# Two-layer graph attention and a transformer layer on one core: the first 1024 nodes' terms made and spread before the mask turns

## The chip, the cores and the metric

The kernel runs on one core of a Trainium2 chip. The metric is device microseconds of one execution. The kernel before has a median of 3264.52 us over three runs (3263.38 to 3267.57).

## The reference, cut to what matters

There are 4096 nodes with 256 features (`x`) and one 4096 x 4096 integer adjacency matrix (`adj`, 64 MB). Two graph attention layers come first, then one transformer layer whose attention uses the same matrix as its mask.

```python
Wh  = jnp.einsum('nd,hdo->hno', x, W)            # W: 8 heads, 256 x 32
src = jnp.einsum('hno,ho->hn', Wh, a[:, :O])
dst = jnp.einsum('hno,ho->hn', Wh, a[:, O:])
e = jax.nn.leaky_relu(src[:, :, None] + dst[:, None, :], 0.2)
alpha = jax.nn.softmax(jnp.where(adj[None] > 0, e, NEG_INF), axis=-1)
out = jnp.einsum('hnm,hmo->hno', alpha, Wh)      # then elu, and x is added
```

The scores of a graph attention layer depend on two numbers per node and head: a source term and a destination term. Because the leaky ReLU has two slopes, the kernel needs for each pair of nodes only the sign of (source term + destination term) and the mask bit. It multiplies sign and mask matrices with values scaled by exponentials of the destination term.

## The kernel before, in words

**Groups.** A graph attention layer is done in 64 groups (`l`, `nb`, `p`, `g`): two blocks `nb` of 1024 destination rows, four pairs of heads `p`, eight column groups `g` of 512 nodes (4 tiles of 128). TensorE's main loop (L1351) multiplies, for each of 8 row tiles and 4 column tiles, the comparison tiles `t8` and the mask tile with the values `vst[g]`.

**What a group needs.** `compare(i)` makes `t8` for group i two groups ahead: four column tiles times two heads, by VectorE (L1086) or ScalarE (L1084), and then one VectorE instruction over 128 x 2048 words, `mask()` (L1099), which puts the mask into them. `compare` reads `s_b`, a tile in which the source terms of 1024 rows are repeated on all 128 partitions. `s_b` comes from `s_fetch` (L1060), two DMAs of 512 KB that read 4 KB rows of the DRAM tensor `s_d` 128 times each. `s_d` is written by `term_rows` (L1031), four DMAs per 512 nodes, after `g_sr` (L1028).

**What makes the terms.** `preparation(l, q)` handles 512 nodes: `features` (L965, L968) transposes the rows, `values(t)` (L978 to L1010) multiplies with `w_ext` and makes the terms and the scaled values, `split(t)` (L1016 to L1019) writes `vst` as two f16 halves with GpSimd's subtraction, and `term_rows` follows. Since a block has 1024 rows, `s_b` for the first group needs `preparation(0, 0)` and `preparation(0, 1)`. `weights_of(l)` (L921 to L941) loads the weights and makes the two term columns of `w_ext`.

**The mask.** `mask_load` (L858) fetches 512 KB of `adj`, `mask_clip` (VectorE, L867) makes bytes of it, `mask_turn` (TensorE L890, ScalarE L892) transposes it, and every second turn is stored to DRAM for later use (L895). Eight such units are the first two column groups; groups 0 to 5 then turn four units each. The loads use three buffers (`g_adj`), so a fourth load waits for a clip.

**Order.** The order on TensorE, ScalarE and VectorE is that of the program, and in `begin()` SyncE's (SP) too. Outside `begin()` a scheduler places SP's DMAs, and can put later ones between those of `begin()`. All DMAs here are issued by SP, in order. In the main loop `beside` places side work between the row tiles of a group. `Norms.__init__` (L1383) loads five small vectors, element by element, as the first DMAs of the program.

Of the kernel before, what the change touches and what calls it, by code (L numbers as in the profile page):

```python
# [751 lines left out]
def graph_attention(  # L752
# [79 lines left out]
    pt = turn_bank([P, HB], F32)  # L832
    nc.tensor.matmul(pt[:, 0:2], once, tiny, start=True, stop=True)
    nc.vector.tensor_scalar(checks.column(), pt[:, 0:1], 2.0**-20, None, op0=ALU.is_equal)
    bits = rows_p.tile([P, P], F16, name="g_rows")
    seen = keep.tile([P, 3], F32, name="g_seen")
    for at, pattern in ((0, 0x38), (32, 0x8000), (64, 0x3880), (96, 0x80)):
        nc.vector.memset(bits[at : at + 32].bitcast(U16), pattern)
# [73 lines left out]
    layers = []  # L912
    coming_rows = {}

    def weights_of(l):

        w, a = weights[l]
        L = Layer()
        L.w_ext = keep.tile([P, DC, D + 2 * H], F32, name="g_w_ext")
        for c in range(DC):  # L920
            nc.sync.dma_start(  # L921
                L.w_ext[:, c, 0:D].rearrange("p (h o) -> p h o", o=O),
                w[:, c * P : (c + 1) * P, :].rearrange("h p o -> p h o"),
            )
        a_sb = ep.tile([P, H, 2, O], F32, name="e_terms")
        nc.sync.dma_start(
            a_sb.rearrange("p h s o -> p (h s o)"), spread(a, [[0, P], [1, H * 2 * O]])
        )
        wa = ep.tile([P, DC, H, O], F32, name="e_x")
        values_ = L.w_ext[:, :, 0:D]  # L930
        terms = L.w_ext[:, :, D:].rearrange("p c (k h) -> p c k h", k=2)
        for k in range(2):
            nc.vector.tensor_tensor(
                wa,
                values_.rearrange("p c (h o) -> p c h o", o=O),
                a_sb[:, :, k, :].unsqueeze(1).to_broadcast([P, DC, H, O]),
                op=ALU.mult,
            )
            nc.vector.tensor_reduce(terms[:, :, k, :], wa, AX.X, ALU.add)
        nc.vector.tensor_scalar(terms[:, :, 1, :], terms[:, :, 1, :], -1.0, None, op0=ALU.mult)  # L940
        nc.vector.tensor_scalar(values_, values_, UP, None, op0=ALU.mult)  # L941
        L.terms = keep.tile([P, 2, NT, H], F32, name=f"g_terms{l}")
        L.negd = L.terms[:, 1]
        L.r = keep.tile([P, NT, H], F32, name=f"g_r{l}")
        L.tops = keep.tile([P, NT], F32, name=f"g_tops{l}")
        L.ft = {}
        layers.append(L)

    def rows_ahead(l, q):
        if q < NG:  # L950
# [3 lines left out]
    def preparation(l, q, bank, first=False):  # L954

        L = layers[l]
        held = {}

        def features(c):

            if c == 0:
                L.ft[q] = stage_p.tile([P, DC, HB], F32, name="g_ft", tag="stage")
            pt = bank()
            for t in range(G):
                nc.tensor.transpose(  # L965
                    pt[:, t * P : (t + 1) * P], coming_rows[l, q][:, t, c * P : (c + 1) * P], ident_f
                )
            nc.scalar.copy(L.ft[q][:, c, :], pt)  # L968
            if c == DC - 1:
                del coming_rows[l, q]  # L970
                if (l, q) != (0, 0) and (l == 0 or q + 1 != NG - 2):
                    rows_ahead(l, q + 1)

        def values(t):
            at = G * q + t
            pv = bank()
            for c in range(DC):
                nc.tensor.matmul(  # L978
                    pv[:, : D + 2 * H],
                    L.ft[q][:, c, t * P : (t + 1) * P],  # L980
                    L.w_ext[:, c, :],
                    start=(c == 0),
                    stop=(c == DC - 1),
                )
            nc.scalar.copy(
                L.terms[:, :, at, :], pv[:, D : D + 2 * H].rearrange("p (k h) -> p k h", k=2)
            )

            big = some.tile([P, 2, H], F32, name="g_big", bufs=4)
            for i, scale in enumerate((-1.0, -LRELU)):  # L990
                nc.scalar.activation(big[:, i, :], pv[:, D + H : D + 2 * H], AF.Exp, scale=scale)
            nc.scalar.activation(L.r[:, at, :], pv[:, D : D + H], AF.Exp, scale=LRELU - 1.0)
            nc.vector.tensor_reduce(
                L.tops[:, at : at + 1], pv[:, :D], AX.X, ALU.max, apply_absolute_value=True
            )

            if l == 0:
# [12 lines left out]
            nc.vector.tensor_scalar(prod[:, :, :, O:], by_head, UP, None, op0=ALU.mult)  # L1010

        def split(t):
            part = held.pop(t).rearrange("p h i v -> p h (i v)")
            halves = vst[q][:, t].rearrange("p h (k v) -> p h k v", k=2)
            if first or t % 2 == 1:
                nc.scalar.copy(halves[:, :, 0, :], part)  # L1016
            else:
                nc.vector.tensor_copy(halves[:, :, 0, :], part)  # L1018
            nc.gpsimd.tensor_tensor(halves[:, :, 1, :], part, halves[:, :, 0, :], op=ALU.subtract)  # L1019

        def term_rows():
# [6 lines left out]
            nc.scalar.copy(sr, pr)  # L1028
            for t in range(G):
                at = (G * q + t) * P  # L1030
                nc.sync.dma_start(s_d[l][:, at : at + P], sr[t * H : (t + 1) * H])  # L1031
# [200 lines left out]

    def begin():

        rows_ahead(0, 0)
        weights_of(0)
        rows_ahead(0, 1)

        units = own[: 2 * 2 * NW]
        del coming[: len(units)]  # L1240
        for k, u in enumerate(units):
# [3 lines left out]
            elif k == 7:  # L1245
                place = t_p.tile([P, 2, G * P], I32, name="t8")
            mask_load(*u, place)
        for q in range(2):
            for k, step in enumerate(preparation(0, q, spare_bank, True)):
                step()  # L1250
                if q == 0 and k in (3, 5, 7, 9):
                    mask_clip(*units[(k - 3) // 2], load=False)
                if q == 1 and k in (2, 4, 6, 8):
                    mask_turn(*units[k // 2 - 1])
                    mask_clip(*units[k // 2 + 3], load=False)
        s_of[0, 0, 0] = s_fetch(0, 0, 0)
        load_ahead(3)
        for k in range(4, len(units)):
            mask_turn(*units[k])
            mask_clip(*turns[0][k - 4])  # L1260
        for i in range(2):
            for step in compare(i):
                step()

    ev = acc = None
    ordered = {mybir.EngineType.PE, mybir.EngineType.Activation, mybir.EngineType.DVE}
# [2 lines left out]
        begin()  # L1269
    for i, (l, nb, p, g) in enumerate(groups):  # L1270
        if l + 1 < NL and nb == 1 and p == 0 and g == NG - 1:
            weights_of(l + 1)
        fetches(i)


# [15 lines left out]
        if i + 2 < len(groups):  # L1291
            steps = compare(i + 2)
            beside(steps[:-1], 0.25 if made else 0.0, 0.95)
            beside(steps[-1:], 0.96, 1.0)
        if i >= len(groups) - NG:
            mine = [step for at, step in handed if at == g]
            beside([lambda step=step: step(lambda: turn_bank([P, HB], F32)) for step in mine], 0.0, 0.9)
# [75 lines left out]
class Norms:  # L1373


    def __init__(self, nc, pool, small, ident, vectors):

        self.nc, self.small, self.ident = nc, small, ident
        self.sb = {}
        for name, src in vectors.items():  # L1380
            self.sb[name] = pool.tile([P, src.shape[0] // P], F32, name=f"n_{name}")
            with nc.allow_non_contiguous_dma(reason="one small vector"):
                nc.sync.dma_start(self.sb[name], src.rearrange("(c p) -> p c", p=P))  # L1383
        self.eps = pool.tile([P, 1], F32, name="n_eps")
        nc.vector.memset(self.eps, LN_EPS)

    def mean(self, xs):
        nc = self.nc
# [55 lines left out]
class Ahead:  # L1444
# [6 lines left out]
        self.xs, self.hn, self.held = {}, {}, {}  # L1451

    def weights(self, bank=None):
        self.w = []
        for c in range(self.D // P):
            self.w.append(self.rows_p.tile([P, self.w_qkv.shape[1]], F32, name="g_adj", bufs=3))
# [540 lines left out]
```

## Time and profile before

| | us |
|---|---|
| median of 3 runs | 3264.52 |
| the profiled execution's own time | 3265.68 |
| its span in the trace | 3263.9 |
| first matmul of the main loop (L1351) | 60.89 |
| stretch 60 to 157: groups 0 to 5, with `preparation` of q = 2 to 7 beside them | about 97 |
| stretch 160 to 840: the rest of graph attention layer 1, TensorE 40.00 of 40 us busy from 200 on | about 680 |

The profiled execution is 1.2 us above the median. A timeline line gives start, duration, engine, line, operation and, in brackets, how long the engine had been idle before it and what released it. SPq is SP's DMA queue; its durations are those of the issue, not of the transfer. A line of the windows view gives busy time of each engine within the stretch, with the number of instructions, and at the end TensorE's granted clock, the DMA engines' share and GB/s.

### The profile page before, as it was taken

To read this page: it belongs to the slowest core of one execution; us is meant where nothing else is said; L and a number is where in the kernel's file an instruction comes from. 1 tells how busy PE (TensorE), PEld (TensorE's weight loads), DVE (VectorE), ACT (ScalarE), POOL (GpSimd) and SP (SyncE) were. 2 spreads that over 40 slices of the span, in tenths; PEclk is the share of its full clock that TensorE was granted. 3 is DMA by queue.
4 is the path that set the end of the run, shared out by engine and by line. 5 is a ranking of instruction groups with operands and counts; after the bars stand their busy time and mean duration, and the time that the engine had idled before them with its cause. 6 is when DMAs were issued, how large, how long until landed. Compare 5 with 4: busy or idle time off the path is not lost.

```text
span 3263.9 us, 139140 instructions
## 1 busy us (share of the span) xinstructions
PE 3098.8 (95%) x64076; PEld 2713.6 (83%) x64076; DVE 2805.1 (86%) x3102; ACT 2703.2 (83%) x3305; POOL 1176.4 (36%) x536
## 2 busy tenths in 40 slices
PE   4899999999889999999988999999999999997999
PEld 3799999999879999999965888888888888885666
DVE  5899999998879999999965999999999999994121
ACT  4799999999779999999974888888888888884332
POOL 1300000000220000000001898899988998893110
PEclk7999999999999999999999999999999999998999
DMA  6666555430311212121136010101011010004200
GB/s 209 193 206 219 159 171 172 145 93 22 99 42 34 93 54 93 37 59 47 38 104 159 14 40 14 39 20 33 27 27 49 11 43 14 20 8 119 70 33 27
DMA packets 210306, 249.30 MB, mean 76 GB/s; under 512 B 87792, under 2 KB 131056, under 8 KB 209712
## 3 DMA queue, kind: packets, MB, share of 16 engines
q1 hardware_dynamic: 209712, 240.31, 24.5%
q8 instruction: 503, 8.24, 1.1%
q14 instruction: 91, 0.75, 0.1%
HBM read 197.80 MB, written 42.47 MB: 74 GB/s over the span
## 4 chain that ended last, share of the span: by engine, by line
PE 44%; ACT 4%; DVE 3%; DMA 2%; issue 1%; POOL 0%; SPq 0%; POOLq 0%; DVEq 0%; ACTq 0%
PE u_ps L1668 14%; PE u_av L1686 14%; PE u_dn L1686 8%; PE misc L1874 3%; ACT t L1084 2%; PE misc L1611 2%; PE misc L1858 1%; DMA u_xres<-rows 1%; PE misc L1630 1%; DVE t L1086 1%; DVE t L1099 1%; PE misc L1432 1%; ACT ln_square L1399 0%; POOL u_xres L1817 0%; PE misc L1822 0%
## 5 line engine op out<-in xcount | busy, mean ns | idle before, releaser
L1351 PE MATMUL bank<-vst,t 128*128 128x132 f16 x16384 | 1451.3, 219 | 54.6 <-DVE t L1099 54.6
L1759 POOL TENSOR_TENSOR u_both<-u_e 128x1024 f32<-128x1024 f32 x448 | 1052.3, 2390 | 933.8 <-DVE u_e L1677 931.8
L1351 PE MATMUL bank<-vst,mask 128*128 128x66 f16 (+1 forms) x10296 | 1345.9, 206 | 0.0
L1084 ACT ACTIVATE t<-s_b,g_terms 128x1024 int8<-128x1024 f32 x1231 | 1318.8, 1155 | 30.9 <-PE bank L1351 21.6
L1351 PEld LDWEIGHTS <-t 128*128 128x128 fp8e4 x16384 | 1184.3, 97 | 69.1 <-DVE t L1099 59.5
L1677 DVE SCALAR_TENSOR_TENSOR u_e<-u_mask,u_ps 128x1024 f32<-128x1024 uint8 x1024 | 1165.8, 1213 | 9.8 <-ACT u_ps L1675 6.3
L1675 ACT ACTIVATE u_ps<-u_ps 128x1024 f32<-128x1024 f32 x1024 | 1030.1, 1009 | 141.5 <-PE u_ps L1668 46.0
L1351 PEld LDWEIGHTS <-mask 128*128 128x128 fp8e4 x10296 | 902.9, 98 | 0.0
L1099 DVE SCALAR_TENSOR_TENSOR t<-mask,t 128x2048 int32<-128x2048 int32 x256 | 591.1, 2309 | 79.9 <-ACT t L1084 69.5
L1668 PE MATMUL u_ps<-u_q,u_k 128*32 128x512 f16 x8192 | 636.0, 382 | 11.7 <-DVE u_e L1677 11.0
L1686 PE MATMUL u_av<-u_e,u_v 128*32 128x128 f32 x16384 | 601.9, 273 | 0.0
L1686 PEld LDWEIGHTS u_av<-u_e,u_v 128*32 128x32 f32 x16384 | 487.4, 110 | 130.5 <-issue 1.2
L1086 DVE TENSOR_SCALAR t<-s_b,g_terms 128x1024 fp8e4<-128x1024 f32 x817 | 582.6, 745 | 0.0
L1019 POOL TENSOR_TENSOR vst<-g_prod,vst 128x528 f16<-128x528 f32 x32 | 38.9, 1232 | 775.8 <-DVE vst L1018 756.8
L1686 PE MATMUL u_dn<-u_both,u_ones 128*32 128x128 f32 x7168 | 279.6, 273 | 0.0
L1668 PEld LDWEIGHTS <-u_k 128*32 128x32 f16 x8192 | 228.3, 95 | 57.8 <-issue 16.2
L1686 PEld LDWEIGHTS u_dn<-u_both,u_ones 128*32 128x32 f32 x7168 | 212.1, 110 | 41.3 <-issue 0.4
L1865 ACT ACTIVATE u_hid<-misc,n_b 128x512 f32<-128x512 f32 x64 | 42.7, 682 | 149.5 <-PE misc L1858 149.4
L1881 DVE TENSOR_TENSOR u_xres<-u_xres,misc 128x256 f32<-128x256 f32 x32 | 13.5, 421 | 121.1 <-PE misc L1874 121.1
L1874 PE MATMUL misc<-u_w,u_hid 128*128 128x256 f32 x512 | 111.8, 379 | 0.0
L1858 PE MATMUL misc<-ln_cols,u_w 128*128 128x512 f32 x256 | 111.2, 592 | 0.0
L1874 PEld LDWEIGHTS misc<-u_w,u_hid 128*128 128x128 f32 x512 | 96.7, 190 | 13.3 <-issue 0.5
(146 smaller groups left out, 1921.3 us busy)
## 6 DMA issues: line engine op xcount, KB each, us to landing
g_adj<-in_adj_dram SPq DMA_DIRECT2D x123, 512.0 KB
mask<-mask SPq DMA_DIRECT2D x128, 256.0 KB
s_b<-s_d SPq DMA_DIRECT2D x64, 512.0 KB
u_mask<-mask SPq DMA_DIRECT2D x32, 512.0 KB
mask<-stage SPq DMA_DIRECT2D x48, 256.0 KB
rows<-e_x SPq DMA_DIRECT2D x32, 256.0 KB
half_d<-u_halves SPq DMA_DIRECT2D x32, 256.0 KB
u_q<-half_d SPq DMA_DIRECT2D x32, 256.0 KB
```

The source lines that it names most:

```text
L1084: nc.scalar.activation(to.bitcast(I8), s, AF.Sign, bias=negd, scale=-1.0)
L1086: nc.vector.tensor_scalar(to, s, negd, -1.0, op0=ALU.is_ge, op1=ALU.mult, saturate=False)
L1099: nc.vector.scalar_tensor_tensor(both, m32.unsqueeze(1).to_broadcast(list(both.shape)), SIGNS, both, op0=ALU.bitwise_or, op1=ALU.bitwise_and,)
L1351: nc.tensor.matmul(to, left, right, start=k not in opened, stop=last)
L1611: nc.tensor.matmul(pq, wq_sb[k][:, i * D + c * P : i * D + (c + 1) * P], hn[:, k, :], start=(k == 0), stop=(k == DC - 1),)
L1668: nc.tensor.matmul(ps[r * O : (r + 1) * O, j, :], k_st[:, h, at : at + O], q_st[:, h, :], start=True, stop=True,)
L1675: nc.scalar.activation(ps, ps, AF.Exp, scale=SCALE)
L1677: nc.vector.scalar_tensor_tensor(e, mask, 0.0, ps, op0=ALU.not_equal, op1=ALU.mult)
L1686: nc.tensor.matmul(to[j * O : (j + 1) * O, at], lefts[j], es[j // 2][:, j % 2, at], start=first and part == 0, stop=last and part == PARTS ...
L1759: nc.gpsimd.tensor_tensor(both, es_of[i - 1][u], es_of[i][u], op=ALU.add)
L1858: nc.tensor.matmul(ph, w1_sb[:, k, f * P : (f + 1) * P], hn[:, k, :], start=(k == 0), stop=(k == DC - 1),)
L1874: nc.tensor.matmul(po[:, :D], hid[:, f, at : at + P], w2_sb[:, f, :], start=(f == 0), stop=(f == FC - 1),)
```

## The change

- `weights_of(l)` becomes `weights_load(l)` (the DMAs, the attention vector first) and `weights_steps(l)` (five VectorE steps, whose products go to a `g_prod` tile and no longer to `e_x`). In layer 1 the five steps are placed one each into groups 0 to 4 of `nb` = 1, `p` = 1; before, all six instructions stood at the start of the last group of `p` = 0.
- `Norms` loads its five vectors in `load()`, called from `Ahead.weights`.
- The test pattern `bits` has its own buffer and no longer one of the two `g_rows` buffers. The rows of q = 0 and q = 1 are loaded one after the other, ahead of the mask loads; those of q = 2 after `s_fetch`.
- `begin()` runs both `features` first, then the weight steps, then the `values` and `split` steps of q = 0 and q = 1 with four clips between them and both `term_rows`, then `s_fetch`. Four mask turns with four clips, `compare(0)`, four turns with four clips, and `compare(1)` follow. The values of q = 1 use `g_prod` tiles (two buffers).

```diff
-    bits = rows_p.tile([P, P], F16, name="g_rows")
+    bits = keep.tile([P, P], F16, name="g_bits")
...
-        rows_ahead(0, 0)
-        weights_of(0)
+        weights_load(0)
+        rows_ahead(0, 0)
         rows_ahead(0, 1)
...
-        for q in range(2):
-            for k, step in enumerate(preparation(0, q, spare_bank, True)):
-                step()
-                if q == 0 and k in (3, 5, 7, 9):
-                    mask_clip(*units[(k - 3) // 2], load=False)
-                if q == 1 and k in (2, 4, 6, 8):
-                    mask_turn(*units[k // 2 - 1])
-                    mask_clip(*units[k // 2 + 3], load=False)
+        first, second = (preparation(0, q, spare_bank, True) for q in range(2))
+        for step in first[:DC] + second[:DC]:
+            step()
+        for step in weights_steps(0):
+            step()
...
+        for step in value[0][:2]:
+            step()
+        for k in range(2):
+            clip(k)
+            value[0][2 + k]()
+        row[0]()
+        for k in range(4):
+            value[1][k]()
+            part[0][k]()
+            if k < 2:
+                clip(2 + k)
+            if k > 1:
+                part[1][k - 2]()
+        row[1]()
         s_of[0, 0, 0] = s_fetch(0, 0, 0)
+        rows_ahead(0, 2)
+        for k in range(4):
+            turn(k)
+            if k < 2:
+                part[1][2 + k]()
+            clip(4 + k)
         load_ahead(3)
+        ahead = turns[0]
+        for step in compare(0):
+            step()
         for k in range(4, len(units)):
-            mask_turn(*units[k])
-            mask_clip(*turns[0][k - 4])
-        for i in range(2):
-            for step in compare(i):
-                step()
+            turn(k)
+            mask_clip(*ahead[k - 4])
+        for step in compare(1):
+            step()
...
         if l + 1 < NL and nb == 1 and p == 0 and g == NG - 1:
-            weights_of(l + 1)
+            weights_load(l + 1)
...
+        if l + 1 < NL and nb == 1 and p == 1 and g < 5:
+            if g == 0:
+                coming_weights = weights_steps(l + 1)
+            beside([coming_weights.pop(0)], 0.3, 0.6)
...
     def weights(self, bank=None):
+        self.norms.load()
```

In the program as built, SP's queue of the opening reads: attention vector, two weight loads, rows of q = 0 and q = 1, eight mask loads, four `s_d` writes, 256 KB of `e_x`, the attention vector of layer 1, four `s_d` writes, four of the five small vectors, two `s_b` loads, rows of q = 2, two mask stores, mask loads. VectorE's order in groups 0 to 5 is the one of before.

More of the change, by code (lines that the diff above doesn't have):

```diff
@@ L913, in graph_attention, with weights_load @@
     coming_rows = {}
-    def weights_of(l):
+    def weights_load(l):
         w, a = weights[l]
         L = Layer()
+        L.a_sb = ep.tile([P, H, 2, O], F32, name="e_terms")
+        nc.sync.dma_start(
+            L.a_sb.rearrange("p h s o -> p (h s o)"), spread(a, [[0, P], [1, H * 2 * O]])
+        )
         L.w_ext = keep.tile([P, DC, D + 2 * H], F32, name="g_w_ext")
@@ L924, in weights_of @@
             )
[L925 to L941, printed above, removed]
         L.terms = keep.tile([P, 2, NT, H], F32, name=f"g_terms{l}")
@@ L947, in weights_of, with weights_steps, step_times, step_sums @@
         layers.append(L)
+    def weights_steps(l):
+        L = layers[l]
+        values_ = L.w_ext[:, :, 0:D]
+        terms = L.w_ext[:, :, D:].rearrange("p c (k h) -> p c k h", k=2)
+        held = {}
+        def step_times(k):
+            wa = some.tile([P, H, 2, V1], F32, name="g_prod").rearrange("p h i v -> p (h i v)")
+            held[k] = wa[:, : DC * D].rearrange("p (c h o) -> p c h o", c=DC, o=O)
+            nc.vector.tensor_tensor(
+                held[k],
+                values_.rearrange("p c (h o) -> p c h o", o=O),
+                L.a_sb[:, :, k, :].unsqueeze(1).to_broadcast([P, DC, H, O]),
+                op=ALU.mult,
+            )
+        def step_sums(k):
+            nc.vector.tensor_reduce(terms[:, :, k, :], held.pop(k), AX.X, ALU.add)
+        def step_ends():
+            nc.vector.tensor_scalar(terms[:, :, 1, :], terms[:, :, 1, :], -1.0, None, op0=ALU.mult)
+            nc.vector.tensor_scalar(values_, values_, UP, None, op0=ALU.mult)
+        steps = []
+        for k in range(2):
+            steps += [lambda k=k: step_times(k), lambda k=k: step_sums(k)]
+        return steps + [step_ends]
     def rows_ahead(l, q):
@@ L970, in features @@
                 del coming_rows[l, q]
-                if (l, q) != (0, 0) and (l == 0 or q + 1 != NG - 2):
+                if (l > 0 or q > 1) and (l == 0 or q + 1 != NG - 2):
                     rows_ahead(l, q + 1)
@@ L995, in values @@
             )
-            if l == 0:
+            if l == 0 and q != 1:
                 if t == 0:
@@ L1247, in begin, with clip, turn @@
             mask_load(*u, place)
-        for q in range(2):
-            for k, step in enumerate(preparation(0, q, spare_bank, True)):
-                step()
-                if q == 0 and k in (3, 5, 7, 9):
-                    mask_clip(*units[(k - 3) // 2], load=False)
-                if q == 1 and k in (2, 4, 6, 8):
-                    mask_turn(*units[k // 2 - 1])
-                    mask_clip(*units[k // 2 + 3], load=False)
-        s_of[0, 0, 0] = s_fetch(0, 0, 0)
+        def clip(k):
+            mask_clip(*units[k], load=False)
+        def turn(k):
+            mask_turn(*units[k])
+        first, second = (preparation(0, q, spare_bank, True) for q in range(2))
[3 more added lines that the diff above has]
+            step()
+        del first[:DC], second[:DC]
+        value = [[steps[k] for k in (0, 1, 3, 5)] for steps in (first, second)]
+        part = [[steps[k] for k in (2, 4, 6, 8)] for steps in (first, second)]
+        row = [steps[7] for steps in (first, second)]
+        for step in value[0][:2]:
+            step()
+        for k in range(2):
+            clip(k)
[9 more added lines that the diff above has]
+        row[1]()
+        s_of[0, 0, 0] = s_fetch(0, 0, 0)
+        rows_ahead(0, 2)
[4 more added lines that the diff above has]
+            clip(4 + k)
         load_ahead(3)
+        ahead = turns[0]
+        for step in compare(0):
+            step()
         for k in range(4, len(units)):
-            mask_turn(*units[k])
-            mask_clip(*turns[0][k - 4])
-        for i in range(2):
-            for step in compare(i):
-                step()
+            turn(k)
+            mask_clip(*ahead[k - 4])
+        for step in compare(1):
+            step()
     ev = acc = None
@@ L1378, in __init__, with load @@
         self.nc, self.small, self.ident = nc, small, ident
-        self.sb = {}
-        for name, src in vectors.items():
-            self.sb[name] = pool.tile([P, src.shape[0] // P], F32, name=f"n_{name}")
+        self.vectors = vectors
+        self.sb = {
+            name: pool.tile([P, src.shape[0] // P], F32, name=f"n_{name}")
+            for name, src in vectors.items()
+        }
+        self.eps = pool.tile([P, 1], F32, name="n_eps")
+        nc.vector.memset(self.eps, LN_EPS)
+    def load(self):
+        nc = self.nc
+        for name, src in self.vectors.items():
             with nc.allow_non_contiguous_dma(reason="one small vector"):
                 nc.sync.dma_start(self.sb[name], src.rearrange("(c p) -> p c", p=P))
-        self.eps = pool.tile([P, 1], F32, name="n_eps")
-        nc.vector.memset(self.eps, LN_EPS)
     def mean(self, xs):
```

## The prediction

> **What bounds the kernel now.** I read the 40 slices first (TensorE is at 9 nearly everywhere, at 4 in the first slice), then windows of the start, then the timeline from 20 to 70 us, the waits of the same stretch, and last the waits of TensorE from 160 to 1100 us, to see whether an earlier start would be kept.
>
> The windows view, busy time of each engine:
>
> ```profile
> 40.00:60.00 20.00, 0.00 (x0) 0.00 (x0) 7.57 (x10) 8.42 (x8) 0.00 (x0) 0.50 0.94 317
> 80.00:100.00 20.00, 16.70 (x196) 14.14 (x197) 16.23 (x27) 13.11 (x42) 5.67 (x5) 1.00 0.71 223
> 240.00:280.00 40.00, 40.00 (x759) 40.00 (x757) 38.84 (x44) 39.95 (x49) 0.00 (x0) 1.00 0.75 226
> ```
>
> From 40 to 60 us TensorE does nothing while the DMA engines are 94% busy. From 80 to 100 nothing is full: groups of 15.4 us, paced by a chain between engines. From about 160 on TensorE is full. So what stands in the opening is the end's loss, one for one, if the later stages keep their length.
>
> The timeline of the opening names the chain:
>
> ```profile
> 24.98 0.40 SPq L743 DMA_DIRECT2D g_rows<-in_x_dram  x1
> 31.80 4.22 SPq L895 DMA_DIRECT2D mask<-mask  x2
> 35.55 0.24 ACT L1028 COPY g_sr<-bank 32x128 f32<-32x128 f32 x1
> 36.11 1.53 SPq L1031 DMA_DIRECT2D s_d<-g_sr  x4
> 38.23 0.45 SPq L743 DMA_DIRECT2D e_x<-in_x_dram  x1
> 38.87 0.92 SPq L1060 DMA_DIRECT2D s_b<-s_d  x2
> 39.83 10.44 SPq L858 DMA_DIRECT2D g_adj<-in_adj_dram  x4
> 47.55 8.42 ACT L1084 ACTIVATE t<-s_b,g_terms 128x1024 int8<-128x1024 f32 x8 [8.41 <-DMA s_b<-s_d]
> 54.43 0.70 DVE L867 TENSOR_SCALAR adj<-g_adj 128x1024 fp8e4<-128x1024 int32 x1 [2.07 <-DMA g_adj<-in_adj_dram]
> 55.04 3.40 DVE L1086 TENSOR_SCALAR t<-s_b,g_terms 128x1024 fp8e4<-128x1024 f32 x5
> 58.54 2.29 DVE L1099 SCALAR_TENSOR_TENSOR t<-mask,t 128x2048 int32<-128x2048 int32 x1
> 60.89 0.40 PE L1351 MATMUL bank<-vst,t 128*128 128x132 f16 x2 [22.38 <-DVE t L1099]
> 62.92 2.29 DVE L1099 SCALAR_TENSOR_TENSOR t<-mask,t 128x2048 int32<-128x2048 int32 x1
> 67.68 0.42 DVE L993 TENSOR_REDUCE g_tops<-turn 128x1 f32<-128x256 f32 x1 [2.46 <-ACT g_r L992]
> ```
>
> The second half of the terms is ready at 35.8, `s_b` lands at 47.55, but VectorE stands in front of four clips and takes the last one's load only at 54.43; only then come its five comparisons and the mask instruction that frees TensorE at 60.89. Two things make this long: the terms come late, and VectorE has clips ahead of the comparisons.
>
> **What the Trainium skill says.** "DMA: Bandwidth & Descriptors", Rules for kernel authors: a DMA that reads what an earlier one wrote has to wait for the first one's semaphore. The trace agrees: the last `s_d` write is issued by 37.64, and `s_b` goes out at 38.87. The same section: a last dimension that isn't contiguous becomes one descriptor per element; the trace has 680 packets for almost no bytes in the first 3.2 us, which are `Norms`' vectors. "GPSIMD Engine Reference", Specifications: its SBUF interfaces are shared with VectorE. The trace agrees: L1010 takes 0.17 us alone and 0.80 beside a `vst` subtraction (at 19.93). "TensorE: Matmul & The Clock Gate", Part 1: the array's clock is halved after idleness; the 0.50 above agrees.
>
> **The change part by part.**
>
> *First transfers.* Before, five small loads stand ahead (0.74 to 3.28 on SP), and the attention vector, issued from 5.08 to 7.49, is what VectorE waits for until 11.28. Now it is first. The weights (256 KB) and it (256 KB) start about 2.7; at the 200 to 390 GB/s of those slices they need some 2.5 us and a receipt, so they land about 6.5. The rows of q = 0, behind them, land about 7.8 (8.12 before). The six weight instructions take 3.1 us, to 9.7; `g_ident_h` (0.19) now stands behind them, and TensorE's test transpose behind that, at 10.0. Then the second features (8 transposes at the 0.2 us of a cold array, 1.6) end at 11.7. The first value matmul starts at 12.0 instead of 14.85: 2.8 us. Bounds: 0 if the weights land late, 4.
>
> *Terms.* From that matmul to the first L993 it was 2.6 us (14.85 to 17.46), so VectorE starts at 14.7. It does six values and four clips before the row that counts can go: a value costs 1.34 us beside GpSimd (0.34 + 0.60 + 0.40), a clip 0.60. ScalarE's `g_sr` of q = 1 stands behind the cast of the sixth value: 14.7 + 6 x 1.34 + 4 x 0.60 = 25.1, and about 0.3 for the cast: `g_sr` at 25.4 instead of 35.55, so 10.1 us. It is earlier because the mask turns of q = 1 and four clips are now behind it.
>
> *SP.* `s_d` goes out at 25.5 to 27.0. Four small vectors follow (4 x 0.5 = 2.0), to 29.0; they hide behind the landing of `s_d`, for which `s_b` waits about 2 us anyway; without that cover they cost 2.0. `s_b` is issued at 29.0 (38.87 before). Then it took 8.7 us, with 768 KB (rows, `e_x`) ahead of it, about 2 us at 350 GB/s; now only the small packets are ahead, about 0.5: 7.3 us, so it lands at 36.3 instead of 47.55: 11.2 us. The mask stores and mask loads are behind it on SP and wait for turns that end by about 30.
>
> *First comparisons.* VectorE is through all eight clips at about 31. It takes 5 comparisons and the mask at once, 5.85 us (55.04 to 60.89): TensorE starts the main loop at 42.2, 18.7 us earlier.
>
> *Second comparisons.* Here part is given back. Four clips for group 0's turns now stand between the two masks. Three loads are there (3 x 0.65 to 44.1); the fourth needs the buffer that the first clip frees at 42.85, and a load takes 4.7 us (the same fourth load was issued at 49.73, when its buffer came free, and landed at 54.43), so 47.55. Clip 0.65, three comparisons 2.0, mask 2.29: 52.5 instead of 65.2, only 12.7 us earlier. The first value of q = 2 on VectorE, which waited for TensorE until 67.68, now waits for this: 52.5. ScalarE gives nearly the same: comparisons from 36.3 (3 x 1.05), four turns (2.1), five comparisons (5.3) to 47.0, then its `g_ft` copy and the 4.4 us that led from there to the value: 51.5. TensorE stalls inside group 0 for it. So the opening is worth 67.7 - 52.5 = **15.2 us**, not 18.7.
>
> *Groups 0 to 5 and after.* Their instruction order is the same; in 62 to 157 us the waits list shows no wait of VectorE for a mask load. Those 97 us are kept, and so is the TensorE-bound stretch after. Cost 0; if mask loads came late there, see the last rival.
>
> *Other edits.* The spread of q = 1 uses two product buffers: its third value waits for GpSimd's subtraction (1.15 us each). By count of casts that is free at about 25 and 27, so 0 to 0.8 us, after `g_sr`, where VectorE has 5 us to spare: 0. The `bits` buffer only lets rows load earlier.
>
> *Layer 1's weights.* Before, VectorE waited 0.97 us for `e_x` at 356.33 and did 3.3 us of steps at once; TensorE then waited 1.5 us:
>
> ```profile
> 364.77 0.29 PE L1351 MATMUL bank<-vst,t 128*128 128x132 f16 x2 [1.50 <-DVE t L1099]
> ```
>
> Now the `e_x` wait is gone and each of five groups gets about 0.7. VectorE is 9.9 of 10 busy there, so pieces may show: between -1.5 and +0.5; I take **-1.0**.
>
> **The sum**: -15.2 - 1.0 = -16.2 us. Against the profiled execution (3265.68, its span 3263.9 and 1.8 around it) 3249.5; against the median, 1.2 lower, **3248.3**.
>
> **Rivals.**
> 1. *The whole first-matmul gain reaches the end.* If the fourth mask load lands by 43.5, the second comparisons end early enough and group 0 keeps its pace: 18.7 + 1.0, or up to 21 if `s_b` alone in the queue takes 5.5 us: about 3244. For it: the DMA queue is emptier. Against: the buffer count of three.
> 2. *Terms or `s_b` gain less.* The weights land no earlier (2.8 less), or the small vectors' packets delay `s_b` by 2 us more, or the fourth load takes 6 us, two of these together: about 11 us remain, 3253.5.
> 3. *It is absorbed.* A later stage waits for something of its own, so the earlier start is lost: 3264. Against: TensorE is full from 200 to 840 and nothing there has a fixed time.
> 4. *Slower.* Mask loads of groups 0 to 5 come late in every group, as SP's queue is denser and the clips come right behind one another. Before, a load is issued at 69.41 and its clip runs at 77.54, a lead of 8.1 us against 4.7 for landing. It decides from a loss of 3.4 us of lead plus 16.2 / 6 = 2.7 us per group; with 4 us of waiting in each of six groups, 24 - 16.2 = +7.8: 3272.
>
> **How the numbers follow.** Forecast 0.62, rival 1 0.13, rival 2 0.17, rival 3 0.04, rival 4 0.04. About 0.2% (6.5 us) is what a measurement of this kernel can tell from no change; so faster 0.92, same 0.04, slower 0.04. The forecast's unknowns (weights 0 to 4 us earlier, a load 4 to 5 us, layer 1's steps -1.5 to +0.5) give 3245 to 3251; to leave out 2 in 10 the range goes a part of the way to rivals 1 and 2: 3243.5 to 3253.5.
>
> **What would show it.** In the profile of the changed kernel: first L993 near 14.7, `g_sr` of q = 1 near 25.4, `s_b` issued near 29 and the first comparison near 36.3, first L1351 near 42.2, the second L1099 ending near 52.5 with TensorE waiting inside group 0, 15.4 us per group to about 142, and no 1.5 us wait near 350. I am wrong if the first L1351 is not before 50, if VectorE waits for `g_adj` in groups 1 to 5, or if the group length changes.

## The result, and the profile after

The changed kernel takes 3249.66 us (median of 6 runs, 3246.16 to 3253.69) beside 3264.64 us for the kernel before (6 runs): ratio 0.9952, 95% interval 0.9939 to 0.9965. Run again beside three of the kernels below (with the label after_again), it took 3247.41 beside 3268.21: 0.9939, interval 0.9925 to 0.9952. The gain is 15 to 21 us; the traces of the first set give 15.5 between the two profiled spans (3263.9 and 3248.4), at a granted TensorE clock of 0.985 in both.

The windows view after (same columns as before):

```profile
40.00:60.00 20.00, 15.18 (x129) 12.90 (x129) 14.29 (x27) 13.05 (x31) 2.70 (x2) 0.71 0.83 281
80.00:100.00 20.00, 17.15 (x205) 14.39 (x203) 16.60 (x30) 13.12 (x41) 8.20 (x4) 1.00 0.66 214
```

In the first line TensorE has 15.18 of 20 us where it had none; in the second the engines are about as busy as before. So the gain is made in the opening. The timeline of the opening, after:

```profile
5.75 0.69 DVE L946 TENSOR_TENSOR g_prod<-g_w_ext,e_terms 128x512 f32<-128x512 f32 x1 [3.77 <-DMA g_w_ext<-in_L_gnn_W_dram]
11.70 4.92 PE L994 MATMUL bank<-g_w_ext,g_ft 128*128 128x272 f32 x16
...
23.60 0.25 ACT L1044 COPY g_sr<-bank 32x128 f32<-32x128 f32 x1
23.87 1.61 SPq L1047 DMA_DIRECT2D s_d<-g_sr  x4
27.62 0.82 SPq L1076 DMA_DIRECT2D s_b<-s_d  x2
34.69 3.23 ACT L1100 ACTIVATE t<-s_b,g_terms 128x1024 int8<-128x1024 f32 x3 [5.07 <-DMA s_b<-s_d]
...
40.30 0.40 PE L1401 MATMUL bank<-vst,t 128*128 128x132 f16 x2 [0.78 <-DVE t L1115]
44.83 0.70 DVE L867 TENSOR_SCALAR adj<-g_adj 128x1024 fp8e4<-128x1024 int32 x1 [2.70 <-DMA g_adj<-in_adj_dram]
45.86 1.11 PE L981 MATMUL turn<-ident,g_rows 128*128 128x128 f32 x4 [2.77 <-ACT g_ft L984]
47.62 2.29 DVE L1115 SCALAR_TENSOR_TENSOR t<-mask,t 128x2048 int32<-128x2048 int32 x1
50.74 0.42 DVE L1009 TENSOR_REDUCE g_tops<-turn 128x1 f32<-128x256 f32 x1 [0.84 <-ACT g_r L1008]
67.14 0.42 DVE L1009 TENSOR_REDUCE g_tops<-turn 128x1 f32<-128x256 f32 x1 [0.59 <-ACT g_r L1008]
```

and, before, the line that answers to the last one:

```profile
83.07 0.42 DVE L993 TENSOR_REDUCE g_tops<-turn 128x1 f32<-128x256 f32 x1 [0.58 <-ACT g_r L992]
```

"The first value of q = 3" stands for this instruction: VectorE's first one for the values of the nodes of q = 3, at the end of group 0.

The first main-loop matmul comes at 40.30 instead of 60.89, 20.6 us earlier; the first value of q = 3 (67.14, before 83.07) only 15.9 earlier. So 4.7 us are given back inside group 0. Two waits stand there: VectorE waits 2.70 us for the fourth mask load, and TensorE waits 2.77 us for a feature copy that ScalarE does behind five comparisons. In the groups that follow nothing is lost: from the first value of q = 3 to the last of q = 7 it takes 135.31 - 67.14 = 68.17 us, before 151.26 - 83.07 = 68.19.

### The profile page after: what moved, and what is told of

Same layout as the page of the kernel before. It is cut to its first block, busy times and chain, and to the rows that moved or that the text cites. A ratio compares the mean times of both kernels' runs of the same rounds, so it can differ in the third digit from the quotient of the medians.

```text
span 3248.4 us, 139142 instructions
## 1 busy us (share of the span) xinstructions
PE 3099.1 (95%) x64076; PEld 2717.4 (84%) x64076; DVE 2804.6 (86%) x3102; ACT 2703.1 (83%) x3305; POOL 1177.5 (36%) x536
## 4 chain that ended last, share of the span: by engine, by line
PE 44%; ACT 4%; DVE 3%; DMA 2%; issue 1%; POOL 0%; SPq 0%; POOLq 0%; DVEq 0%; ACTq 0%
PE u_ps L1725 15%; PE u_av L1743 14%; PE u_dn L1743 8%; PE misc L1931 3%; ACT t L1100 2%; PE misc L1668 2%; PE misc L1915 1%; PE misc L1687 1%; DMA u_xres<-rows 1%; DVE t L1102 1%; DVE t L1115 1%; PE misc L1488 1%; ACT ln_square L1455 0%; POOL u_xres L1874 0%; PE misc L1879 0%
## 5 line engine op out<-in xcount | busy, mean ns | idle before, releaser
L1725 PEld LDWEIGHTS <-u_k 128*32 128x32 f16 x8192 | 228.6, 95 | 57.4 <-issue 16.2
```

The source lines that it names most:

```text
L1725: nc.tensor.matmul(ps[r * O : (r + 1) * O, j, :], k_st[:, h, at : at + O], q_st[:, h, :], start=True, stop=True,)
```

## The experiments

The time of a kernel scatters by several us between its own runs (3246.45 to 3252.49 for the second set of the changed kernel), so beside each median I read milestones in the trace, one trace per kernel. V0 is the first `g_tops` (VectorE's first value); it varies from 12.74 to 14.18 in kernels whose work up to there is the same. "q3 - V0" is the time from V0 to the first value of q = 3. The medians come from several chips; each ratio is to the kernel before, run beside that kernel on its chip.

| kernel | V0 | first mask instruction | first value q = 2 | first value q = 3 | q3 - V0 | median us | ratio to before, interval |
|---|---|---|---|---|---|---|---|
| before | 17.46 | 58.54 | 67.68 | 83.07 | 65.61 | 3264.64 | |
| changed | 14.18 | 37.95 | 50.74 | 67.14 | 52.96 | 3249.66 | 0.9952 (0.9939 to 0.9965) |
| after_again | 13.99 | 37.86 | 51.23 | 66.94 | 52.95 | 3247.41 | 0.9939 (0.9925 to 0.9952) |
| e1_clips_first | 12.79 | 46.87 | 55.09 | 70.49 | 57.70 | 3255.26 | 0.9968 (0.9957 to 0.9980) |
| e2_old_transfers | 18.71 | 42.17 | 54.86 | 70.28 | 51.57 | 3252.35 | 0.9965 (0.9953 to 0.9976) |
| e4_turns_inside | 12.82 | 43.40 | 55.98 | 71.77 | 58.95 | 3254.89 | 0.9970 (0.9958 to 0.9983) |
| e3_weights_at_once | 13.63 | 37.67 | 50.92 | 66.06 | 52.43 | 3248.20 | 0.9949 (0.9933 to 0.9966) |
| e11_products_in_e_x | 13.52 | 37.03 | 49.96 | 65.86 | 52.34 | 3250.45 | 0.9949 (0.9935 to 0.9963) |
| e5_fourth_buffer | 13.16 | 36.89 | 49.15 | 64.68 | 51.52 | 3249.90 | 0.9953 (0.9940 to 0.9967) |
| e6_features_first | 13.80 | 37.56 | 50.15 | 65.22 | 51.42 | 3248.47 | 0.9949 (0.9936 to 0.9963) |
| e7_both | 14.13 | 38.23 | 50.03 | 65.10 | 50.97 | 3247.14 | 0.9949 (0.9936 to 0.9963) |
| e8_both_at_once | 12.74 | 36.34 | 48.15 | 63.22 | 50.48 | 3246.16 | 0.9942 (0.9928 to 0.9955) |
| e9_vectors_behind | 14.09 | 35.72 | 49.47 | 64.62 | 50.53 | 3247.39 | 0.9937 (0.9924 to 0.9951) |
| e10_all | 13.73 | 35.10 | 48.74 | 64.48 | 50.75 | 3248.57 | 0.9942 (0.9928 to 0.9956) |

Where an edit touches the work up to V0 itself (e2 and e4), the first value of q = 3 counts, not the difference. Four traces with the opening of the changed kernel (its own two, e3 and e11) have a q3 - V0 of 52.34 to 52.96, so a difference of 0.6 us tells nothing.

The expectations on record follow word for word; all diffs are against the changed kernel. That of the changed kernel run again:

> The changed kernel itself once more, as the neighbour of the three kernels beside it: 3249.7, the first value of q = 2 between 49.5 and 50.8 us in the trace.

Its median came 2.3 below, and the first value of q = 2 at 51.23, 0.4 outside: the same program differs by this much from itself.

**Which part carries the gain.** Three kernels undo one part each.

e1_clips_first: the four mask turns and clips come ahead of the first comparisons again.

```diff
-        for step in compare(0):
-            step()
         for k in range(4, len(units)):
             turn(k)
             mask_clip(*ahead[k - 4])
-        for step in compare(1):
-            step()
+        for i in range(2):
+            for step in compare(i):
+                step()
```

> The changed kernel with compare(0) put back behind the last four turns and clips; terms and transfers stay early. Theory (each of the changed orders carries a part): s_b still lands near 34.7, but VectorE takes the four clips first; the fourth load can start only when the first clip has freed its buffer (about 38.7) and takes 4.7, so the clips end near 44; five comparisons and the mask (5.85) put the first L1401 near 49.9 instead of 40.3, the first value of q = 2 near 56.7 (6.8 after it, as before the change) instead of 50.7, and the end 6 us later than the changed kernel: about 3255.5. Rival (the gain is the early terms alone, the clips' place costs nothing since their loads are there in time): first L1401 within 2 us of 40.3 and the end within 1 us of the changed kernel.

Its timeline:

```profile
33.51 8.42 ACT L1100 ACTIVATE t<-s_b,g_terms 128x1024 int8<-128x1024 f32 x8 [2.43 <-DMA s_b<-s_d]
37.61 0.70 DVE L867 TENSOR_SCALAR adj<-g_adj 128x1024 fp8e4<-128x1024 int32 x1 [7.83 <-DMA g_adj<-in_adj_dram]
...
42.76 0.70 DVE L867 TENSOR_SCALAR adj<-g_adj 128x1024 fp8e4<-128x1024 int32 x1 [1.76 <-DMA g_adj<-in_adj_dram]
...
49.22 0.40 PE L1400 MATMUL bank<-vst,t 128*128 128x132 f16 x2 [18.77 <-DVE t L1115]
```

`s_b` is there at 33.51, but VectorE waits for the loads of the clips until 42.76. The first main-loop matmul comes at 49.22 (49.9 expected), 8.9 us later than in the changed kernel. At q = 3 that is 3.4 us (4.7 from V0), in the median 5.6. So the earlier first matmul is worth about half of itself; the rest is what group 0 gives back in the changed kernel and not here: from the first matmul to the first value of q = 3 it takes 21.3 us here, 22.2 before and 26.8 in the changed kernel.

e4_turns_inside: terms, clips and turns interleaved as before, the other parts kept.

```diff
-        for step in first[:DC] + second[:DC]:
-            step()
         for step in weights_steps(0):
             step()
...
+        for q, steps in enumerate((first, second)):
+            for k, step in enumerate(steps):
+                step()
+                if q == 0 and k in (3, 5, 7, 9):
+                    clip((k - 3) // 2)
+                if q == 1 and k in (2, 4, 6, 8):
+                    turn(k // 2 - 1)
+                    clip(k // 2 + 3)
```

> The changed kernel with the terms made as before: q = 0, then q = 1 with its features, mask turns and clips between its values, and the mask stores ahead of the second s_d writes on SP; early transfers and compare(0) ahead of the last clips stay. Theory: from the first value matmul to g_sr of q = 1 it takes 20.7 us again instead of 11.9, so g_sr comes near 32.4, s_b is issued near 36.4, and the first L1401 is near 49.1; the end is about 8.8 us later than the changed kernel: about 3258.5. Rival (the loads of the mask bound the opening, so early terms only wait for them): first L1401 within 3 us of 40.3.

The direction was right and the size too large: `s_b` goes out at 33.59, 6.0 later, the first matmul starts at 45.75, 5.5 later, q = 3 is 4.6 later, the median 5.2. From V0 to `g_sr` of q = 1 it does take 8.2 us more (17.65 instead of 9.42); but V0 is 1.4 earlier here, since the features of q = 1 no longer stand ahead of it or by scatter, and no small vectors stand between `s_d` and `s_b`, which saves 1.2.

e2_old_transfers: small vectors first, rows ahead of weights, attention vector last.

```diff
-        weights_load(0)
         rows_ahead(0, 0)
+        weights_load(0)        # in it, the attention vector behind the weights
...
         nc.vector.memset(self.eps, LN_EPS)
+        self.load()            # in Norms.__init__
...
-        self.norms.load()      # in Ahead.weights
```

(The remarks behind `#` are added here.)

> The changed kernel with the first transfers as before: five small vectors, then the rows of q = 0, the weights and the attention vector; bits keep their own buffer. Theory: the attention vector lands near 11.3 again, the weight steps end near 14.4, and the first value matmul starts near 14.6 instead of 11.7; all of the opening is 2.9 us later (g_sr of q = 1 near 26.5, first L1401 near 43.2) and so is the end: about 3252.5. Rival (the small vectors, which stand between s_d and s_b in the changed kernel, cost there what they no longer cost at the head): s_b is issued within 1 us of 27.6 and the end is within 1 us of the changed kernel.

```profile
12.59 0.69 DVE L946 TENSOR_TENSOR g_prod<-g_w_ext,e_terms 128x512 f32<-128x512 f32 x1 [10.50 <-DMA e_terms<-in_L_gnn_a_dram]
28.84 1.67 SPq L1047 DMA_DIRECT2D s_d<-g_sr  x4
31.66 0.82 SPq L1076 DMA_DIRECT2D s_b<-s_d  x2
38.91 3.23 ACT L1100 ACTIVATE t<-s_b,g_terms 128x1024 int8<-128x1024 f32 x3 [4.32 <-DMA s_b<-s_d]
```

VectorE waits for the attention vector to 12.59 instead of 5.75, and the first value matmul comes at 16.10 (14.6 expected, 11.70 in the changed kernel), which shows as V0 at 18.71. At q = 3 3.1 us are left of this, in the median 2.7.

Undone one by one, the three parts are worth 3.4 + 4.6 + 3.1 = 11.1 us at q = 3, of 15.9 together. If e1 is counted from V0, which its edit doesn't touch, it is 4.7 and the sum 12.4. What is left is no more than a few us, and each part's figure carries the scatter of V0 (up to 1.4), so whether a part is worth more in company of the others is not shown. The medians can't decide it: the intervals of the three ratios overlap that of the changed kernel's first set. What shows that each part counts are the waits in the traces.

**The opening's queue.** `s_b` has to wait until `s_d` has landed. In e2 and e4, where no small vectors stand between, `s_b` is issued 1.15 and 1.25 us after the end of the last `s_d` issue; in the changed kernel 27.62 - 25.48 = 2.14. e9_vectors_behind issues them behind `s_b`:

```diff
         s_of[0, 0, 0] = s_fetch(0, 0, 0)
+        SMALL[0]()        # Norms.load
         rows_ahead(0, 2)
...
     def weights(self, bank=None):
-        self.norms.load()
```

> The five small vectors are issued behind the two s_b loads instead of four of them ahead, all else as in the changed kernel. Theory A (only part of their issue is hidden: in two kernels without them there, s_b went out 1.15 and 1.25 us after the end of s_d's issue, against 2.14 in the changed kernel): s_b is issued 0.9 to 1.0 us earlier relative to s_d, the first main-loop matmul and the end come 0.9 earlier, 3248.8. Rival B (the step as predicted: they hide wholly behind the landing of s_d): no change, 3249.7. Rival C (their packets also slow s_b): 2 us or more, 3247.5.

Its timeline:

```profile
23.64 1.38 SPq L1047 DMA_DIRECT2D s_d<-g_sr  x4
26.36 0.82 SPq L1076 DMA_DIRECT2D s_b<-s_d  x2
32.46 3.23 ACT L1100 ACTIVATE t<-s_b,g_terms 128x1024 int8<-128x1024 f32 x3 [3.08 <-DMA s_b<-s_d]
35.72 2.29 DVE L1115 SCALAR_TENSOR_TENSOR t<-mask,t 128x2048 int32<-128x2048 int32 x1 [0.52 <-ACT t L1100]
```

From the start of `s_d`'s issue to that of `s_b`'s it is 2.72 us (3.75 in the changed kernel, 2.82 in e2, 2.56 in e4): with the vectors ahead `s_b` goes out about 1.0 later. From there to the landing of the second half it is 6.10 (7.07), another 1.0. The first mask instruction follows V0 after 21.63 instead of 23.77, and 2.4 are left at q = 3. By its size this is rival C; but its reason, that the vectors' packets slow `s_b`, is not what the traces show. In e2 no vector stands ahead of `s_b`, and it still took 38.91 - 31.66 = 7.25 us to land. What e9 also changes is what follows: behind the five vectors the first mask load goes out 6.9 us after `s_b`, in the changed kernel 3.1, in e2 3.3. That these transfers share the DMA engines with `s_b`, and that it lands earlier without them, is likely but was not tried alone. So of the 2 us, 1.0 is the price of the vectors ahead of `s_b`, shown by three kernels; the other 1.0 comes with e9's order, and its cause stays open. The medians of the two kernels run side by side (3247.39 and 3247.41) show neither; 2 us are too few for them.

**Group 0.** e5_fourth_buffer gives the fourth mask load a buffer of its own:

```diff
         ahead = turns[0]
+        mask_load(*coming.pop(0), mask_p.tile([P, 2, G * P], I32, name="mask"))
...
-            mask_clip(*ahead[k - 4])
+            mask_clip(*ahead[k - 4], load=k > 4)
```

> The fourth mask load of group 0's four units gets a buffer of its own (the first of the four clips then loads nothing), so it needn't wait for the first clip. Theory A (ScalarE's order sets when group 0's first value starts): VectorE's 2.70 us wait for the fourth load goes, the second mask instruction ends near 47.2 instead of 49.9, but the first value of q = 2 stays at 50.7 behind ScalarE's g_ft copies (45.24 and 47.02), and the time stays at 3249.7, within 0.7. Rival B (the step as the prediction had it: the clip and the second mask on VectorE set it): the first value comes 2.5 us earlier, near 48.2, and the time is 3247.2.

```profile
42.01 0.70 DVE L867 TENSOR_SCALAR adj<-mask 128x1024 fp8e4<-128x1024 int32 x1 [0.60 <-DMA mask<-in_adj_dram]
44.79 2.29 DVE L1115 SCALAR_TENSOR_TENSOR t<-mask,t 128x2048 int32<-128x2048 int32 x1
49.15 0.42 DVE L1009 TENSOR_REDUCE g_tops<-turn 128x1 f32<-128x256 f32 x1 [2.06 <-ACT g_r L1008]
```

The second mask ends at 47.08, but VectorE now waits 2.06 us for ScalarE, so the first value of q = 2 gains 0.6 from V0 on, not 2.5; the two traces of the changed kernel differ by as much (36.56 and 37.24). As theory A says, ScalarE stands right behind. In the second trace of the changed kernel it is the other way round:

```profile
46.24 0.70 DVE L867 TENSOR_SCALAR adj<-g_adj 128x1024 fp8e4<-128x1024 int32 x1 [3.96 <-DMA g_adj<-in_adj_dram]
49.02 2.29 DVE L1115 SCALAR_TENSOR_TENSOR t<-mask,t 128x2048 int32<-128x2048 int32 x1
51.23 0.42 DVE L1009 TENSOR_REDUCE g_tops<-turn 128x1 f32<-128x256 f32 x1
```

There the clip of the fourth load came 1.4 us later, and the value follows the mask without a gap. So the two chains end close together (0.84 us apart in the first trace), and which is last depends on when a load lands.

e6_features_first puts both `features` of q = 2 ahead of `compare(1)`, e7_both does this and the buffer, e8_both_at_once adds layer 1's steps at once, and e10_all the small vectors behind `s_b`.

```diff
+        early = prepared_early[0] = preparation(0, 2, lambda: turn_bank([P, 512], F32))
+        for step in early[:DC]:
+            step()
+        del early[:DC]
         for step in compare(1):
             step()
...
```

> The two features steps of q = 2 (8 transposes, 2 g_ft copies) move from group 0 to ahead of the second comparisons; the mask loads stay as they are. Theory A: g_ft is there by 41.5 and TensorE's 2.77 us wait for it at 45.86 goes; ScalarE's five comparisons then end near 46.4 and VectorE's second mask, still behind the fourth load, at 49.9; so the first value of q = 2 comes at 50.0 instead of 50.74, a gain of 0.8: 3248.9. Rival B (VectorE alone sets it): the first value stays at 50.7, no change. Rival C (only TensorE's order counts): the first value near 47, a gain of 3.5: 3246.

> Both edits of the two kernels ahead of this one together. Theory A: the two waits cover one another, so only together do they bring something: the second mask, now behind ScalarE's last comparison at 46.4, ends near 48.7, the first value of q = 2 comes near 48.8 and the time falls by 2.0 against the changed kernel: 3247.7. Rival B (the fourth load alone mattered): as much as that edit alone. Rival C (group 0 is set by what follows, at the lower clock of TensorE): under 0.5.

> As the one ahead, with layer 1's weight steps at once where they are loaded instead of spread over five groups. Theory A: the spreading is worth nothing, so the gain of 2.0 stays and at most 1 more comes: 3246.7 to 3247.7. Rival: the steps at once cost 1.0 to 1.5 of waiting by TensorE near layer 1's loads: 3249.

> Fourth mask load in its own buffer, features of q = 2 ahead of the second comparisons, layer 1's weight steps at once, and the small vectors behind s_b. Theory A: the separate gains add: 2.3 in the opening, 1.0 by the vectors, 0 to 1 at layer 1's steps, 3245.4 to 3246.4, and 3.3 to 4.3 below the changed kernel beside it. Rival: group 0 is set by VectorE and TensorE's low clock, so that the earlier s_b is lost again: 3247.

In e6 the first value gained only 0.2 from V0 (0.8 expected), but q3 - V0 fell by 1.5, as it did by 1.4 in e5: each edit alone brings most of what both bring (2.0 in e7), so that they work "only together" was wrong. e8, with the same opening as e7, has 50.48. e9's edit alone gives 50.53, and all together in e10 50.75: the gains don't add, as the rival of e10 had it. It named TensorE's low clock as the reason. The clock is low there (0.50 in e10 from 48 to 51 us, and in the changed kernel from the start of the main loop to 51), but no run separates it. A line of e10's waits shows what is next:

```profile
PE turn L994 <- ACT mask L892: 3.4, 1, 3.4
```

TensorE waits here at 45.47 for its second value matmul, because the bank is still to be copied by ScalarE behind its comparisons; the next mask turn then waits 2.09 us for VectorE's first product, which stands behind the second mask. None of these versions is shown to be faster than the changed kernel: the lowest median is that of e8 (ratio 0.9942), inside the two intervals of the changed kernel.

**Layer 1's weights.** Layers are counted from 0 in the program, so layer 1 is the second one. e3_weights_at_once does the five steps in one place again, with the new product buffer; e11_products_in_e_x does that with the products in `e_x`.

```diff
             weights_load(l + 1)
+            for step in weights_steps(l + 1):
+                step()
...
-            wa = some.tile([P, H, 2, V1], F32, name="g_prod").rearrange("p h i v -> p (h i v)")
+                held["wa"] = ep.tile([P, DC, H, O], F32, name="e_x")        # e11 only
```

> The changed kernel with all weight steps of layer 1 at the start of the last group of p = 0, nb = 1, as before, but into a g_prod tile, so that they don't wait for e_x. Theory: TensorE waits for L1115 1 to 1.5 us near 350 instead of 0.8 in two waits, and the end is 0.2 to 0.7 us later than the changed kernel, not measurable by the clock but by the trace. Rival (the spreading is worth 2 us or more): TensorE waits 3 us there.

> Layer 1's weight steps at once, where they are loaded, and their products in the e_x buffer as in the kernel before (layer 0's too). Theory A (the wait for the e_x buffer was what cost TensorE 1.5 us before, not that the steps stand together): VectorE waits about 1 us for a row store that reads e_x, TensorE then 1.2 to 1.5 us, the time is 1.0 above the kernel with steps at once and products apart: 3249.2. Rival (less slack in the order of before): no wait on e_x, TensorE waits 0.3, 3248.2.

Waits between 300 and 420 us (total in us, times, longest), of e3:

```profile
PE bank L1399 <- DVE t L1115: 0.3, 1, 0.3
```

and of e11:

```profile
PE bank L1400 <- DVE t L1116: 2.1, 1, 2.1
DVE e_x L947 <- DMA rows<-e_x: 1.5, 1, 1.5
```

The steps at once cost TensorE 0.3 us, less than the changed kernel's spread (0.8 in two waits); the expectation of e3 was wrong there. Put the products back into `e_x`, and VectorE waits 1.5 us for a row store that still reads it, and TensorE 2.1. So it is the buffer that took the wait away, not the spreading. e11's median is 3250.45 (ratio 0.9949, 0.9935 to 0.9963), e3's 3248.20, from another chip; 2 us are within the scatter.

## Why the prediction was right

The forecast was 3248.3, the median is 3249.66. That the two are so close is in part luck: they differ by 1.4 us, the two medians of the changed kernel by 2.3, and misses in several steps cancelled. By its steps:

- *First transfers.* First value matmul foreseen at 12.0, measured 11.70; first value on VectorE 14.7 and 14.18. e2 shows that the order of the transfers does this (12.59 instead of 5.75 for the first weight step). V0 alone is no close test, since it scatters by 1.4.
- *Terms.* `g_sr` of q = 1 foreseen at 25.4, measured 23.60. Half a microsecond is the earlier start. The rest is the price of a value: 14.18 to 23.54, where the seventh value starts, holds six values and four clips at 0.60, so (9.36 - 2.40) / 6 = 1.16 us each and not 1.34, because only one of them was slowed: L1026 took 0.89 us once (at 19.40, just after GpSimd's first subtraction began at 19.11) and 0.17 to 0.26 in the other five. The waits of q = 1's last two values for a product buffer (0.70 us at 24.65, 0.78 at 26.86) fell behind `g_sr`, as foreseen for one.
- *SP.* This step failed in a term. The four small vectors were costed at nothing on the queue, hidden behind "about 2 us" in which `s_b` waits for `s_d` anyway. That cover is smaller: the lines of before that the prediction shows have 38.87 - 37.64 = 1.23 us from the end of `s_d`'s issue to `s_b`, e9 has 1.34. So the vectors cost about 1.0 (e9). The half us that the prediction put on their packets is not theirs either: `s_b` took 7.07 us (7.3 foreseen), but 7.25 in e2 without them. In the sum the miss did not show, since `g_sr` was 1.8 earlier than thought: `s_b` went out at 27.62 (29.0 foreseen). Here two misses cancel, which is luck.
- *First comparisons.* 5.61 us from landing to the first matmul (34.69 to 40.30), 5.85 foreseen; 40.30 against 42.2, and e1 shows that it is the clips' place that makes it.
- *Second comparisons.* This was the step that decided between the forecast and rival 1. The fourth load did come late, 44.83 (47.55 foreseen, as everything was some 2 us earlier), 4.0 us after the first clip had freed its buffer. VectorE and ScalarE do end close together, as it said. Foreseen was a gain of 15.2 up to the first value of q = 2; it is 16.9 there, and 15.9 at q = 3. Rival 1 did not come true: of the 20.6 us at the first matmul, 4.7 did not get past group 0. e5 to e7 show that the fourth load and the feature copies are part of this: take one away and 1.4 or 1.5 us come back, with both 2.0. Where the other 2.7 us go is not shown. The first value matmul of q = 2 (at 48.12) took 2.16 us at a granted clock of 0.50, before (at 66.06) 1.16 at 1.00, so the clock may have a part in it.
- *Groups 0 to 5.* Their length is kept (68.17 us from q = 3 to q = 7, before 68.19), and VectorE has no wait for a mask load in 52 to 145 us: rival 4 (late mask loads) did not happen. Nor did rival 3, since the transformer's first score matmul, at 1755.2 instead of 1770.2, is still 15.0 earlier.
- *Layer 1's weights.* -1.0 foreseen, -0.7 measured (TensorE's waits there 1.5 and 0.8). The cause named first, the `e_x` wait, is the right one; the spread has no worth (e3).
- *Not foreseen.* By the first value of layer 1 the gain is 841.41 - 824.82 = 16.6 us, just what the two steps above give (15.9 + 0.7). By that layer's last value it is 966.44 - 951.80 = 14.6, and it stays near that: 15.0 at the first score matmul, 15.5 between the spans. The 2.0 us are lost in one group, from the first value of q = 2 to that of q = 3 of layer 1: 14.2 us, before 12.5. In it TensorE's granted clock (the third figure from the end) falls in the changed kernel and not before:

```profile
850.00:853.00 3.00, 3.00 (x17) 2.39 (x17) 3.00 (x3) 0.64 (x5) 0.24 (x1) 0.53 0.87 249
866.60:869.60 3.00, 3.00 (x28) 2.39 (x29) 3.00 (x3) 0.90 (x9) 0.11 (x1) 1.00 0.98 343
```

  The first line is of the changed kernel, the second the same place before; TensorE does 17 matmuls in 3 us instead of 28. The same fall stands in the second trace of the changed kernel and in e1, e3 and e5, in e4 some 12 us later, and in this stretch of e2 and e6 to e11 not at all. What decides it was not tried. Its absence goes with a part of the lead of e6 to e10: they stand 4.0 to 5.5 us ahead of the changed kernel at the first score matmul (counted from V0), of which only 1.5 to 2.5 us are there at q = 3.

  The prediction thus had the opening 0.7 us too small, layer 1's weights 0.3 too large, and nothing for this loss: 16.2 foreseen, 15.0 to 15.5 by the traces.

## What to carry to other kernels

Where an opening waits for one small result that has to go through DRAM, make that result first. Put nothing on its queue ahead of the read back, beyond what fits into the wait for the write. Put the instruction that feeds the busiest engine ahead of those that wait for bulk loads. Count an earlier start only at the first point where two engines' chains meet again: here 20.6 us at the first matmul were 15.9 one group later. And before crediting a spread of work, look whether the stall was for the work or for its buffer.

## What was not expected of the hardware

- Four vectors of 1 KB, loaded element by element, delayed the issue of a 1 MB read behind them by 1.0 us. Between 20 and 40 us the changed kernel has 2280 packets under 512 bytes and e2, without the vectors there, 1231: about one packet for each of their 1024 elements.
- The 1 MB read itself, a 4 KB row to each of 128 partitions in two DMAs, moves slowly in its middle while the DMA engines are well busy, with the vectors ahead of it (changed kernel, first line) and without (e2, second line):

```profile
31.00:32.00 1.00, 0.00 (x0) 0.00 (x0) 0.65 (x2) 0.00 (x0) 0.00 (x0) 0.50 0.65 139
35.00:36.00 1.00, 0.22 (x3) 0.10 (x1) 1.00 (x2) 0.00 (x0) 0.13 (x1) 0.50 0.68 131
```

  That is 139 and 131 GB/s at a share of 0.65 and 0.68; four to five us later, in the mask loads, the same traces reach 412 and 408 GB/s. So the vectors are not what makes it slow. Its time from issue to landing was 7.0 to 7.6 us where rows, mask stores and mask loads were issued close behind it, 6.55 in e4 without the stores, and 6.10 and 5.88 in e9 and e10, where the vectors stood between.
- The stretch from the first score matmul to the end, with the same instructions in every variant, took from 1491.9 us (e11) to 1497.3 us (e6) in single traces. This scatter is larger than the effect of every edit to group 0, and it is why their medians can't be told apart and milestones were read instead.
